# Paged attention with a conditional mix: other places for the new keys' second value products, the mix product and the weight loads

## The chip, the cores and the metric

The kernel runs on one core of a Trainium2 chip. The metric is the device time of one execution in microseconds (us). The engines of the core are named as the profile names them: PE (TensorE, matrix products), DVE (VectorE), ACT (ScalarE), POOL (GpSimd) and SP (SyncE, which here only issues transfers). Each has its own queue of instructions and works it off in order; they wait for each other through semaphores. SP, ACT and POOL each issue DMA transfers, in the order of their own instructions. [...]

## The reference, cut to what matters

```python
def _L0_cond_ref(x, weights, condition):             # x [64, 32, 512], weights [16, 32, 32]
    W = weights[condition]
    return jnp.einsum('bct,bcd->bdt', x, W)

def _L1_cond_ref(x, Wq, Wk, Wv, Wo, q_norm_w, k_norm_w, k_cache, v_cache, block_table, cache_seqlens):
    q = jnp.einsum('bsd,ed->bse', x, Wq).reshape(bsz, seqlen, HQ, D)     # 32 heads of 128
    k = jnp.einsum('bsd,ed->bse', x, Wk).reshape(bsz, seqlen, HK, D)     # 8 heads of 128
    v = jnp.einsum('bsd,ed->bse', x, Wv).reshape(bsz, seqlen, HK, D)
    q = _rope(_rmsnorm(q, q_norm_w), pos);  k = _rope(_rmsnorm(k, k_norm_w), pos)
    kc = k_cache[block_table].reshape(bsz, L, HK, D)                     # L = 512 cached keys
    vc = v_cache[block_table].reshape(bsz, L, HK, D)
    k_all = jnp.concatenate([kc, k], axis=1);  v_all = jnp.concatenate([vc, v], axis=1)
    scores = jnp.einsum('bqhd,bkhd->bhqk', q, repeat(k_all)) * SCALE     # masked by cache_seqlens
    o = jnp.einsum('bhqk,bkhd->bqhd', softmax(scores), repeat(v_all))
    return jnp.einsum('bse,de->bsd', o.reshape(bsz, seqlen, HQ * D), Wo)

x = x + _L0_cond_ref(x, L0_cond_weights, itok_B_0_15)
x = x + _L1_cond_ref(x, Wq, Wk, Wv, Wo, q_norm_w, k_norm_w, k_cache, v_cache, itok_Bx16_0_63, itok_B_207_1644)
```

All is float32. There are 64 batches of 32 tokens with 512 features. Each batch first mixes its 32 tokens by a 32x32 matrix that its condition picks out of sixteen ("the mix"), and then attends over 512 cached keys, which lie in pages, and its own 32 new ones.

## The kernel before

**Steps and batches.** A tile is 128 rows: four batches (BT = 4) of 32 tokens. There are 16 tiles (NT), and each is worked twice, once for each half of the heads (NHH = 2; 4 key heads, so 16 query heads, in a half): 32 steps. Steps 0 to 15 are the first half, 16 to 31 the second. The first half mixes x and stores its transpose and its sum in DRAM; the second loads them. A step runs its four batches one after the other (variable bt), and a batch its four key heads (variable g): 16 slots, slot = 4 bt + g.

**What a slot does.** The loop is at L834 to L892. Each slot has the scores of its own head against the cached keys (scores, L523: 4 products into ps, then an exponential on ACT into pr) and the value products of the head before (values, L579: 4 products into po; after each second head DVE adds the new keys' part nv, takes the reciprocal of the denominators and scales: L597 to L600). In between lie pieces of the next step (pieces, L803: mix and transpose of x, projections, norm and rotation, transposes) and of this one: new_scores (L538) in slot 0, new_values (L555) for heads 0 and 1 in slot 1 and for heads 2 and 3 in slot 3, and in slot 3 the output product of the step before (out_proj, L468, 32 products of 512 columns).

**Buffers in PSUM.** ps and po have two buffers each. Everything else on PE, the mix (pmix), x's transposes (px1t), projections (pp), their transposes (pt), new scores (psn), new values (pnv) and the output (pout), shares the tag "pp" with BT = 4 buffers. One call of new_values takes all four (one per batch); ACT copies each of them into nv (L577). nv has one buffer per step, so the first copies of a step wait until DVE has used the last values of the step before.

**Cached keys and values.** Keys come by SP as k_t, 16 transfers of 64 KB a batch, two batches deep (load_k, L265), issued when a Batch is made, two batches ahead. DVE copies one head of the following batch in each slot (head_keys, L514, into kh, four buffers). Values are gathered by POOL's indirect DMA (fetch, L296, into raw, three buffers), and ACT masks them into the batch's buffer (fill, L506 and mask_v, L313). Four fills come in slot 3 of each step, one in most others.

**Weights.** Each tag has one buffer. Wq, Wk, Wv of the second half are loaded in step 14 from slot 11 (L870), Wo of the first half in step 0, slots 9 to 12, Wo of the second in step 16, slots 12 to 15 (L868), all on SP's queue.

**The order of work.** PE's and SP's instructions run in the order of the program text (manual_schedule, L88). From the loop on, ACT, DVE and POOL are ordered by the scheduler of the framework, which follows the text by priority and by when it takes an instruction to be ready. Before the loop (L671 to L801, "the opening") all engines follow the text.

**The opening.** bd is a 128x128 matrix with the four 32x32 condition matrices on its diagonal; the mix product of a tile is bd against x. load_cond_weights (L241) loads the four condition numbers of a tile into registers and issues four transfers of 4 KB; in the opening it does so on ACT's queue.

Of the kernel before, what the change touches and what calls it, by code (L numbers as in the profile page):

```python
# [11 lines left out]
F32 = mybir.dt.float32  # L12
I32 = mybir.dt.int32
AF = mybir.ActivationFunctionType
ALU = mybir.AluOpType
# [4 lines left out]
P = 128  # L20
B, S, HID = 64, 32, 512
D, HQ, HK = 128, 32, 8
REP = HQ // HK
# [32 lines left out]
def cond_resid_paged_attention_kernel(  # L56
# [34 lines left out]


    cond_row = const.tile([1, NT, BT], I32, tag="cond", name="cond_row")
    lens_sb = const.tile([P, NT], I32, tag="lens", name="lens_sb")
    freq = const.tile([P, HD], F32, tag="freq", name="freq")
    norm_w = {}
# [88 lines left out]
    def steps_of(exact, pools):  # L185
# [34 lines left out]

        wt = {}

        def load_w(kind, hh, g=0):
            if kind == "q":
                src = wq[:, (hh * QH + g * REP) * D : (hh * QH + (g + 1) * REP) * D]
            elif kind == "o":
                src = wo[(hh * QH + g * REP) * D : (hh * QH + (g + 1) * REP) * D, :]
            else:
                src = (wk if kind == "k" else wv)[:, hh * GH * D : (hh + 1) * GH * D]
            t = wpool.tile(  # L230
                [P, 4, 512], F32, tag=f"w{kind}{g}", name=f"w{kind}{g}_{hh}_{uid}"
            )
            wt[kind, hh, g] = t
            if kind == "o" and not exact:
                src = src.rearrange("(h j p) e -> h p j e", h=REP, p=S)
                for h in range(REP):
                    nc.sync.dma_start(t[h * S : (h + 1) * S, :, :], src[h])
                return
            nc.sync.dma_start(t, src.rearrange("(c p) e -> p c e", p=P))

        def load_cond_weights(t, eng=nc.sync, kind=mybir.EngineType.SP):  # L241
            _, number = nc.values_load_multi_w_load_instructions(
# [99 lines left out]
        def x1_c(st):  # L342
            if st.hh:
                return
            pm = ps_p.tile([P, 512], F32, tag="pp", name=f"pmix_{st.name}")
            nc.tensor.matmul(pm, bd, st.acc, start=True, stop=True)  # L346
            nc.vector.tensor_tensor(st.acc, pm, st.acc, ALU.add)
# [322 lines left out]

        steps = [Step(n) for n in range(NHH * NT)]  # L671
        if not exact:
            nc.scalar.dma_start(cond_row, cond.rearrange("(i s) t -> s t i", s=S)[0:1])
            nc.gpsimd.dma_start(pages_sb, pages)
            nc.gpsimd.dma_start(norm_w["q"], qn_w.partition_broadcast(P))
            nc.gpsimd.dma_start(norm_w["k"], kn_w.partition_broadcast(P))
# [37 lines left out]
        load_w("q", 0, 0)  # L714
        nc.scalar.dma_start(lens_sb, lens)
        nc.scalar.dma_start(freq, inv_freq.partition_broadcast(P))
        load_cond_weights(0, nc.scalar, mybir.EngineType.Activation)
        load_w("k", 0)
        load_w("q", 0, 1)
        load_w("q", 0, 2)  # L720
# [81 lines left out]

        def pieces(st):  # L803
            do = {
                0: (x1_a, x1_c),
                3: (x1_b,),
                4: (k_a, (q_a, 0)),
                5: ((q_a, 1),),
                6: (v_a, k_b, (q_b, 0)),
                8: ((q_a, 2), (q_b, 1)),  # L810
                10: ((q_a, 3), (q_b, 2)),
                13: ((q_b, 3),),
            }
            if st is second:
                do[4], do[6] = ((q_a, 0),), (k_b, (q_b, 0))
            return do
# [17 lines left out]
        for st in steps:  # L834
# [4 lines left out]
            for bt in range(0 if st.n else 1, BT):  # L839
                this = batch  # L840
                for g in range(GH):
# [2 lines left out]
                        scores(this, g)  # L844
                    if slot == 0:
                        new_scores(st)
                    if slot == 1:
                        new_values(st, 0)
                    for piece in fill.get(slot, ()):
                        if isinstance(piece, tuple):  # L850
                            piece[0](ahead, piece[1])
                        else:
                            piece(ahead)
                    if slot == 3:
                        out_proj(steps[st.n - 1])
                        new_values(st, 2)
                        if st.n + 1 < NT // TRIG:
                            tmp = work.tile(
                                [P, 3, TRIG * HD], F32, tag="w1", name=f"trig_{st.n}"
                            )  # L860
# [110 lines left out]
```

## Time and profile before

| | |
|---|---|
| median of 4 runs (lowest to highest) | 2281.05 us (2277.68 to 2283.19) |
| the profiled execution: time, span | 2277.57 us, 2275.8 us |
| TensorE's granted clock, mean | 0.994 |
| PE busy in output products (L474), projections of q (L390) | 445.7, 460.6 us |
| PE busy in scores (L527), values (L585) | 542.5, 550.4 us |
| PE busy in new values (L569), mix (L346) | 62.2, 19.6 us |
| ACT busy in fills (L316), in exponentials (L535) | 361.7, 304.8 us |
| moved by DMA, mean rate | 318.13 MB, 140 GB/s |

The span is the time from the first to the last instruction of the profiled execution. Busy shares are averages over the span. A line of the timeline has the start and the length of an instruction or of a run of them in us, the engine, the line of the kernel, the operation, output and inputs, shape and count, and in brackets the idle time of the engine before it and what ended it. In a line of the list of waits stand the total, the number and the longest of the waits of one line for one other. Matrix products are pipelined: the starts of successive ones tell what one costs.

### The profile page before, as it was taken

To read this page: it belongs to the slowest core of one execution; us is meant where nothing else is said; L and a number is where in the kernel's file an instruction comes from. 1 tells how busy PE (TensorE), PEld (TensorE's weight loads), DVE (VectorE), ACT (ScalarE), POOL (GpSimd) and SP (SyncE) were. 2 spreads that over 40 slices of the span, in tenths; PEclk is the share of its full clock that TensorE was granted. 3 is DMA by queue.
4 is the path that set the end of the run, shared out by engine and by line. 5 is a ranking of instruction groups with operands and counts; after the bars stand their busy time and mean duration, and the time that the engine had idled before them with its cause. 6 is when DMAs were issued, how large, how long until landed. Compare 5 with 4: busy or idle time off the path is not lost.

```text
span 2275.8 us, 41860 instructions
## 1 busy us (share of the span) xinstructions
PE 2231.9 (98%) x13590; PEld 1566.1 (69%) x13590; DVE 1075.5 (47%) x2717; ACT 942.9 (41%) x1726; POOL 771.8 (34%) x1005
## 2 busy tenths in 40 slices
PE   8999999999999999999999999999999999999998
PEld 5766677666776667766677766677666777666775
DVE  4544455444454444554444544445534455444452
ACT  3444444444443344433344434344333444333442
POOL 3423333323333233332333323333333343333331
PEclk9999999999999999999999999999999999999999
DMA  7844454344443444435657444544344544344442
GB/s 220 198 131 126 138 150 128 110 132 139 143 135 115 136 136 139 138 119 160 206 150 185 143 121 129 150 139 138 113 134 132 148 148 121 112 137 142 144 134 68
DMA packets 364486, 318.13 MB, mean 140 GB/s; under 512 B 46737, under 2 KB 308881, under 8 KB 364257
## 3 DMA queue, kind: packets, MB, share of 16 engines
q1 hardware_dynamic: 320064, 176.53, 27.1%
q0 software_dynamic: 41136, 134.55, 19.6%
q10 hardware_dynamic: 3056, 4.27, 0.5%
q8 instruction: 110, 1.80, 0.3%
q14 instruction: 120, 0.97, 0.2%
HBM read 302.59 MB, written 12.58 MB: 138 GB/s over the span
## 4 chain that ended last, share of the span: by engine, by line
PE 88%; DMA 4%; DVE 3%; SPq 2%; issue 1%; ACT 1%; ACTq 0%; POOL 0%; DVEq 0%
PE pout_x L474 19%; PE pp_q_x L390 18%; PE po_x L585 18%; PE ps_x L527 17%; PE pp_v_x L390 5%; PE pp_k_x L390 5%; PE pt_q_x L434 2%; PE pnv_x L569 2%; SPq L279 2%; DMA raw_x<-in_vc_dram,v_row 1%; DMA wo_x<-in_wo_dram 1%; PE psn_x L545 1%; PE pmix_x L346 1%; PE pt_k_x L434 1%; DMA k_t_x<-in_kt_dram 1%
## 5 line engine op out<-in xcount | busy, mean ns | idle before, releaser
L303 POOL DMA_INDIRECT raw_x<-in_vc_dram,v_row x512 | 511.4, 999 | 675.3 <-ACT v_x L316 622.1
L585 PE MATMUL po_x<-v_x,pr_x 128*128 128x129 f32 x4096 | 550.4, 277 | 3.3 <-ACT pr_x L535 3.3
L527 PE MATMUL ps_x<-qt_x,kh_x 128*128 128x128 f32 x4096 | 542.5, 275 | 5.5 <-DVE kh_x L520 3.8
L585 PEld LDWEIGHTS po_x<-v_x,pr_x 128*128 128x128 f32 x4096 | 504.6, 192 | 51.3 <-issue 36.1
L527 PEld LDWEIGHTS ps_x<-qt_x,kh_x 128*128 128x128 f32 x4096 | 500.2, 192 | 7.9 <-issue 4.9
L535 ACT ACTIVATE pr_x<-ps_x 128x512 f32<-128x512 f32 x512 | 304.8, 600 | 379.7 <-PE ps_x L527 377.0
L390 PE MATMUL pp_q_x<-wq_x,x1t_x 128*128 128x512 f32 x1024 | 460.6, 592 | 0.0
L474 PE MATMUL pout_x<-wo_x,ot_x 128*128 128x512 f32 x1024 | 445.7, 593 | 2.9 <-ACT nv_x L577 2.7
L316 ACT ACTIVATE v_x<-raw_x,valid 128x512 f32<-128x512 f32 x512 | 361.7, 720 | 110.8 <-DMA raw_x<-in_vc_dram,v_row 110.3
L474 PEld LDWEIGHTS pout_x<-wo_x,ot_x 128*128 128x128 f32 x1024 | 191.9, 190 | 233.3 <-issue 229.1
L390 PEld LDWEIGHTS pp_q_x<-wq_x,x1t_x 128*128 128x128 f32 x1024 | 187.1, 190 | 198.5 <-issue 198.2
L520 DVE COPY kh_x<-k_t_x 128x512 f32<-128x512 f32 x506 | 215.9, 429 | 203.9 <-PE ps_x L527 113.1
L577 ACT COPY nv_x<-pnv_x 128x258 f32<-128x258 f32 x256 | 77.3, 388 | 341.2 <-PE pnv_x L569 276.4
L400 ACT ACTIVATE sq_q_x<-pp_q_x 128x512 f32<-128x512 f32 x128 | 76.5, 597 | 298.8 <-issue 133.1
L404 DVE TENSOR_REDUCE ms_q_x<-sq_q_x 128x4 f32<-128x512 f32 x128 | 87.3, 682 | 199.7 <-ACT sq_q_x L400 199.7
L407 POOL TENSOR_TENSOR rs_q_x<-ms_q_x,minus_half 128x4 f32<-128x4 f32 x128 | 132.5, 1035 | 129.9 <-DVE ms_q_x L405 129.7
L379 POOL TENSOR_TENSOR cw_k_x<-norm_k,cos 128x64 f32<-128x64 f32 x32 | 10.1, 315 | 442.1 <-DVE ms_k_x L405 442.1
L597 DVE TENSOR_TENSOR nv_x<-po_x,nv_x 128x258 f32<-128x258 f32 x256 | 107.5, 420 | 100.7 <-PE po_x L585 91.6
L411 DVE TENSOR_TENSOR rope_q_x<-pp_q_x,cw_q_x 128x512 f32<-128x512 f32 x128 | 87.3, 682 | 102.6 <-PE pt_k_x L434 102.6
L390 PE MATMUL pp_v_x<-wv_x,x1t_x 128*128 128x512 f32 x256 | 115.2, 592 | 0.0
L390 PE MATMUL pp_k_x<-wk_x,x1t_x 128*128 128x512 f32 x256 | 115.2, 592 | 0.0
L600 DVE TENSOR_TENSOR o_x<-nv_x,rden 128x256 f32<-128x256 f32 x256 | 107.8, 421 | 3.3
(95 smaller groups left out, 1426.1 us busy)
## 6 DMA issues: line engine op xcount, KB each, us to landing
k_t_x<-in_kt_dram SPq DMA_DIRECT2D x2048, 64.0 KB
wq_x<-in_wq_dram SPq DMA_DIRECT2D x8, 1024.0 KB
raw_x<-in_vc_dram,v_row POOLq DMA_INDIRECT x512, 3.9
wo_x<-in_wo_dram SPq DMA_DIRECT2D x32, 256.0 KB
xt_x<-in_x_dram SPq DMA_DIRECT2D x16, 256.0 KB
x1t_d<-x1t_x ACTq DMA_DIRECT2D x16, 256.0 KB
acc_d<-xt_x SPq DMA_DIRECT2D x16, 256.0 KB
acc_x<-acc_d SPq DMA_DIRECT2D x16, 256.0 KB
```

What stands on the lines that cost most here:

```text
L303: nc.gpsimd.indirect_dma_start(out=raw.rearrange("p g d -> p (g d)"), out_offset=None, in_=vc, in_offset=bass.IndirectOffsetOnAxis(ap=v_ro ...
L316: nc.scalar.activation(v_bufs[b % 2][:, c, :, 0:D], raw, AF.Copy, scale=ok)
L390: nc.tensor.matmul(pp, st.x1t[:, c, :], w[:, c, :], start=(c == 0), stop=(c == KC - 1))
L404: nc.vector.tensor_reduce(ms, sq, AX.X, ALU.add)
L407: nc.gpsimd.tensor_tensor(rs, ms, minus_half, ALU.pow)
L474: nc.tensor.matmul(po, st.ot[:, i, :], wt["o", st.hh, i // 4][:, i % 4, :], start=(i == 0), stop=(i == QH - 1),)
L520: last["dve"] = nc.vector.tensor_copy(k, ba.k_raw[:, :, g, :]).ins
L527: nc.tensor.matmul(ps[:, c, :], ba.k[g][:, c * P : (c + 1) * P], queries(ba, g), start=True, stop=True,)
L535: last["act"] = nc.scalar.activation(pr, ps, AF.Exp, scale=SCALE).ins
L585: nc.tensor.matmul(ba.po[:, g % 2, :], ba.pr[g][:, c, :], ba.v_t[:, c, g, :], start=(c == 0), stop=(c == VC - 1),)
L597: nc.vector.tensor_tensor(t, ba.po, t, ALU.add)
L600: nc.vector.tensor_tensor(ba.o[:, both, :], t[:, :, 0:D], rd.unsqueeze(2).to_broadcast([P, 2, D]), ALU.mult,)
```

## The change

Four things are done.

- new_values for heads 2 and 3 is called ahead of the other pieces of slot 3, and not behind the output product. In slots 0 to 3 the value products of the head before come ahead of the pieces, and not at the end of the slot. The mix product of the next step (x1_c) moves from slot 0 to the end of slot 2, and x's transposes (x1_b) stand in slot 3 behind the value products.
- load_w takes a part of a tile, and load_parts loads one half of a weight tile per slot. Wo is loaded in slots 4 to 11 of steps 0 and 16; Wk, Wq, Wv of the second half in slots 5 to 15 of step 14 and slot 0 of step 15.
- The mix weights of the first tile come by one indirect DMA on POOL: row numbers are computed on DVE from the first column of the conditions, the gather brings 128 rows of 32 values, and four copies (two on DVE, two on ACT) place them in bd.
- cond_row, which the other tiles' condition numbers are read from, is loaded on ACT's queue behind these copies.

```diff
+    cond_0 = const.tile([P, 1], I32, tag="cond_0", name="cond_0")
...
-        def load_w(kind, hh, g=0):
+        def load_w(kind, hh, g=0, part=slice(0, 4)):
...
-            t = wpool.tile(
-                [P, 4, 512], F32, tag=f"w{kind}{g}", name=f"w{kind}{g}_{hh}_{uid}"
-            )
-            wt[kind, hh, g] = t
+            if part.start == 0:
+                wt[kind, hh, g] = wpool.tile(
+                    [P, 4, 512], F32, tag=f"w{kind}{g}", name=f"w{kind}{g}_{hh}_{uid}"
+                )
+            t = wt[kind, hh, g]
...
-                for h in range(REP):
+                for h in range(part.start, part.stop):
                     nc.sync.dma_start(t[h * S : (h + 1) * S, :, :], src[h])
                 return
-            nc.sync.dma_start(t, src.rearrange("(c p) e -> p c e", p=P))
+            nc.sync.dma_start(t[:, part, :], src.rearrange("(c p) e -> p c e", p=P)[:, part, :])
+
+        def load_parts(which, hh, at):
+
+            if 0 <= at < 2 * len(which):
+                load_w(which[at // 2][0], hh, which[at // 2][1], slice(at % 2 * 2, at % 2 * 2 + 2))
...
-            nc.scalar.dma_start(cond_row, cond.rearrange("(i s) t -> s t i", s=S)[0:1])
+            nc.scalar.dma_start(cond_0, cond[:, 0:1])
+            nc.vector.tensor_scalar(cond_0, cond_0, float(S), row, ALU.mult, ALU.add)
...
-        load_cond_weights(0, nc.scalar, mybir.EngineType.Activation)
+        w_sel = work.tile([P, S], F32, tag="o", name="w_sel", bufs=1)
+        nc.gpsimd.indirect_dma_start(
+            out=w_sel,
+            out_offset=None,
+            in_=w_cond,
+            in_offset=bass.IndirectOffsetOnAxis(ap=cond_0, axis=0),
+        )
+        for i in range(BT):
+            blk = slice(i * S, (i + 1) * S)
+            (nc.scalar.copy if i % 2 else nc.vector.tensor_copy)(bd[blk, blk], w_sel[blk, :])
+        nc.scalar.dma_start(cond_row, cond.rearrange("(i s) t -> s t i", s=S)[0:1])
...
             do = {
-                0: (x1_a, x1_c),
-                3: (x1_b,),
+                0: (x1_a,),
...
-                    if slot == 1:
-                        new_values(st, 0)
+                    if slot in (1, 3):
+                        new_values(st, slot - 1)
+                    if slot < GH and valued is not None:
+                        values(*valued)
                     for piece in fill.get(slot, ()):
...
+                    if slot == 2 and ahead:
+                        x1_c(ahead)
                     if slot == 3:
+                        if ahead:
+                            x1_b(ahead)
                         out_proj(steps[st.n - 1])
-                        new_values(st, 2)
...
-                    if st.n == 0 and 9 <= slot < 13 or st.n == NT and slot >= 12:
-                        load_w("o", st.hh, (slot - 9 if st.n == 0 else slot - 12))
-                    if st.t == NT - 2 and st.hh + 1 < NHH:
-                        if slot == 11:
-                            load_w("k", st.hh + 1)
-                            load_w("v", st.hh + 1)
-                        if slot in (12, 13):
-                            for i in range(2):
-                                load_w("q", st.hh + 1, 2 * (slot - 12) + i)
+                    if st.t == 0:
+                        load_parts([("o", i) for i in range(GH)], st.hh, slot - GH)
+                    if st.n in (NT - 2, NT - 1):
+                        load_parts(
+                            [("k", 0), ("q", 0), ("q", 1), ("v", 0), ("q", 2), ("q", 3)],
+                            1,
+                            slot - 5 + (st.n - NT + 2) * BT * GH,
+                        )
...
-                    if valued is not None:
+                    if slot >= GH and valued is not None:
                         values(*valued)
```

More of the change, by code (lines that the diff above doesn't have):

```diff
@@ L853, in steps_of @@
                             piece(ahead)
+                    if slot == 2 and ahead:
+                        x1_c(ahead)
                     if slot == 3:
+                        if ahead:
+                            x1_b(ahead)
                         out_proj(steps[st.n - 1])
-                        new_values(st, 2)
                         if st.n + 1 < NT // TRIG:
-                            tmp = work.tile(
-                                [P, 3, TRIG * HD], F32, tag="w1", name=f"trig_{st.n}"
-                            )
+                            tmp = work.tile([P, 3, TRIG * HD], F32, tag="w1", name=f"trig_{st.n}")
                             with tc.issue_after(last["dve"]), tc.issue_after(last["act"]):
```

## The prediction

> **What bounds the kernel now.** I read the busy shares first, then TensorE's waits, then the order of time in one ordinary step and in the places that the waits point to. Busy shares:
>
> ```profile
> PE 2231.9 (98%) x13590; PEld 1566.1 (69%) x13590; DVE 1075.5 (47%) x2717; ACT 942.9 (41%) x1726; POOL 771.8 (34%) x1005
> ```
>
> TensorE (PE) sets the time. The change neither adds nor removes a matmul, so it can only act on time in which PE stands or is slow: 44 us of the 2275.8 us span look idle. TensorE's list of waits, at its places:
>
> ```profile
> PE pmix_x L346 <- DMA bd<-in_w_cond_dram: 8.0, 1, 8.0
> PE pnv_x L569 <- DVE xt_x L481: 5.7, 16, 0.4
> PE pnv_x L569 <- DVE acc_x L481: 5.3, 15, 0.4
> PE ps_x L527 <- DVE kh_x L520: 3.8, 1, 3.8
> PE po_x L585 <- ACT pr_x L535: 3.3, 1, 3.3
> ```
>
> Each edit aims at one of these. The second and third come once in every step from 1 on. The timeline of step 8 (PE's rows, slot 1 above, slot 3 below the dots):
>
> ```profile
> 604.91 1.06 PE L527 MATMUL ps_x<-qt_x,kh_x 128*128 128x128 f32 x8
> 605.89 0.73 PE L569 MATMUL pnv_x<-vn_x,pn_x 32*128 32x129 f32 x16
> 606.55 1.16 PE L585 MATMUL po_x<-v_x,pr_x 128*128 128x129 f32 x8
> 607.55 1.06 PE L527 MATMUL ps_x<-qt_x,kh_x 128*128 128x128 f32 x8
> ...
> 610.66 13.90 PE L474 MATMUL pout_x<-wo_x,ot_x 128*128 128x512 f32 x32
> 624.49 0.50 PE L569 MATMUL pnv_x<-vn_x,pn_x 32*128 32x129 f32 x6
> 625.35 0.71 PE L569 MATMUL pnv_x<-vn_x,pn_x 32*128 32x129 f32 x10 [0.36 <-DVE xt_x L481]
> 625.98 1.16 PE L585 MATMUL po_x<-v_x,pr_x 128*128 128x129 f32 x8
> 626.98 1.06 PE L527 MATMUL ps_x<-qt_x,kh_x 128*128 128x128 f32 x8
> ```
>
> Start to start, the same sixteen matmuls take 0.66 us in slot 1 and 1.49 us in slot 3: new_values takes all four "pp" buffers of PSUM (BT = 4), and the fourth still holds the output product until VectorE (DVE) has added it. So 0.83 us are lost, twice what the wait list books.
>
> The end of step 0, all engines but the weight loads:
>
> ```profile
> 102.52 1.06 PE L585 MATMUL po_x<-v_x,pr_x 128*128 128x129 f32 x8
> ...
> 106.78 1.43 DVE L520 COPY kh_x<-k_t_x 128x512 f32<-128x512 f32 x4 [3.86 <-DMA wo_x<-in_wo_dram]
> 107.36 2.05 PE L527 MATMUL ps_x<-qt_x,kh_x 128*128 128x128 f32 x8 [3.78 <-DVE kh_x L520]
> 109.33 1.94 PE L545 MATMUL psn_x<-qt_x,kn_x 128*32 128x128 f32 x32
> ```
>
> The keys of the next batch stood behind 4 MB of Wo on SP's queue, and after the wait PE ran slowly (psn 1.94 us against 1.08 in step 8).
>
> **New keys (steps 1 to 31).** I call t0 the start of a step's slot-0 scores (start of psn less 0.98 us) and L the time after t0 at which DVE copies the first keys of batch 1. DVE is in order, and this copy waits for k_t. In step 4:
>
> ```profile
> 323.58 0.69 DVE L347 TENSOR_TENSOR xt_x<-pmix_x,xt_x 128x512 f32<-128x512 f32 x1 [3.31 <-PE pmix_x L346]
> 327.45 0.43 DVE L520 COPY kh_x<-k_t_x 128x512 f32<-128x512 f32 x1 [3.18 <-DMA k_t_x<-in_kt_dram]
> 328.96 1.21 ACT L577 COPY nv_x<-pnv_x 128x258 f32<-128x258 f32 x4 [2.94 <-DVE o_x L600]
> ```
>
> Behind that copy stands the normalising of the last batch, and only then may ScalarE (ACT) overwrite nv and free the four buffers of slot 1's new_values. L is 7.0 us here; over steps 2 to 14 it is 5.2 to 7.0, mean 6.4; over 16 to 31 5.4 to 7.5 where it shows.
>
> Before, PE goes from pout's start to slot 4's scores in 13.75 us of product and a 2.57 us tail (624.41 to 626.98). After, the tail's work stands ahead of pout at slot 1's pace: 0.75 new_values with its gap, 0.99 values.
>
> Steps whose successor is in the second half (15 to 31, no mix): pout starts at t0 + 8.31 when nothing waits, so 8.31 + 2.57 = 10.88 becomes 8.31 + 1.74 = 10.05: 0.83 us saved. If L is late, slot 1's copies end at L + 2.3 (step 19: L 6.2, ended at 8.5), the new product at L + 2.75, values at L + 3.75; for L = 7.5 that is 11.25, against 9.57 + 2.57 before (step 23). The saving stays 0.8 to 0.9. 17 steps by 0.83: **14.1 us**.
>
> Steps 1 to 14: the mix product moves from slot 0 to the end of slot 2, and with it its DVE sum. There it asks for a pp buffer while slot 1's new_values holds all four. Copies start L + 1.05 (as in step 19, where the order in slot 0 is already the new one), the first is out at L + 1.45. Then mix 0.97, scores 0.89, new_values 0.75, values 0.99, x transposes 0.44: pout at L + 5.5. The fourth pnv tile also waits for the mix's sum, which stands on DVE behind the copies and the normalising of slot 2 (about L + 3.9 at its end); I add 0.2. L + 5.7 with L = 6.4 is 12.1; before, 9.60 + 2.57 = 12.17. So **0**: the old wait is paid, the new one takes its place. Bounds per step: 0.83 gained (nothing waits), 1.1 lost (the sum stands behind one more key copy and L is 7.0).
>
> ACT is the other cover: pout (or the x transposes) now needs a copy of slot 3's new values, and four v fills are ready in the same slot. In slot 0 one fill already goes ahead of the copy of psn's result. A fill takes 0.62 of ACT's time (two in a row: 1.33, one: 0.71); in a second-half step with one ahead, the first copy ends at scores' end + 0.69 + 0.62 + 0.39 = 1.7 us, when values has ended too (1.74). One is free; each further one costs 0.62. I take one; bounds none and four.
>
> **Wo in halves.** In step 0 the 16 transfers go to slots 4 to 11. SP stands still from 60.3 to 66.4 us with the DMA share at 0.03 (60 to 65), so 2 MB fit before batch 3's keys; the other 2 MB follow them, and batch 4's keys can be issued from about 84 instead of 86.8 to 102, needed at 94 by DVE. Without the stall psn would start at 104.4 instead of 109.33 and the next po, now at 112.91, at 106.28: **6.6 us**. In step 16 the same 16 transfers delay v's gathers (5.6 us wait on ACT, then 3.3 on PE); the distance from that pout to the next is 73.71 against 68.86: **4.85 us**. Now they are spread over about 37 us of long slots. Cover gone (keys or gathers late all the same): both stay, 11.5 us.
>
> **Wk, Wv, Wq** go in twelve halves over slots 5 to 15 of step 14 and slot 0 of 15. Before, step 15 loses 0.78 us (69.64 against 68.86). Behind the halves on SP stand batch 3's and the next step's keys; the last 2 MB come just ahead of those for batch 1 of step 15. I take 0.4 saved; bounds 0.8 saved, 5 lost (2 MB at 296 GB/s are 7 us, 2 of them in time that SP has).
>
> **The opening.** Removed: four register loads and four 4 KB transfers on ACT's queue, whose last lands at 15.6. Added: a 512 B column, one DVE operation (0.15 us, like the row computation on a 128x1 tile), a gather, four 32x32 copies (each under a 128x128 DVE operation's 0.23 or ACT's 0.40). The column lands about 4.5 to 5.5 (cond_row was read at 3.9; lens, later, landed at 7.2), the gather is issued by 6.8 (1 us on POOL). Its landing is not in the trace: bounds 3.9 (median of v's gathers over the whole run) and 8.5 (lens_at, issued among the same loads), and I take 6.5, nearer to the latter for its place: 13.3, bd at 13.7, 2 us sooner.
> [...]
> Behind the waiting gather on POOL stand pages_at and lens_at: issued at 7 instead of 3.4, landing by 15.5, needed at 19.0. Behind the copies on DVE stands the first angle table, which can't start before 11.55 anyway, and the mix's sum behind it; cond_row's second use on ACT is at 22.1. Then batch 0's keys, issued until 31.05, and Wv, issued at 31.1, meet a PE that comes sooner, so I keep **1 us**; bounds 5 saved, 2 lost.
>
> Sum: 14.1 + 0 + 6.6 + 4.85 + 0.4 + 1 = 27 us. The profiled execution took 2277.57 us (span 2275.8), so it would be 2250.6; it was 3.5 below the median of the runs shown, 2281.05, so the median goes to **2254 us**.
>
> **Rivals.**
> A. Steps 1 to 14 gain too (L falls, or the copies come sooner): 14 by 0.83 more is 11.6: 2242. For it: L below 5.7 in steps 9, 12 and 13. Against: ten others.
> B. Two or three fills ahead of the copies on ACT: the 17 steps lose 0.62 or 1.24 each, 14 more about 0.4: 2270 to 2281. For it: raws for three fills wait in slot 3, and after x's copy three fills do run in a row there. Against: that copy went ahead of them.
> C. The halves only move the stall: 11.5 back, 2265.
> D. Slower: all four fills ahead. The fourth waits for a gather started by the first (step 8: it ends 16.1 us after t0, step 18: 14.4), so pout starts 0.4 later: 4.3 lost in 14 steps, 3.9 in 17, together 127 against 13 saved elsewhere: 2395. It decides from the third fill on, where the steps lose more than they gain. Against: its gather lands long after the new product.
>
> **How the numbers follow.** Chances: forecast 0.45 (2248 to 2261), A 0.17, B 0.18, C 0.08, D 0.12. Range 2240 to 2276: it leaves out D, the top of B and the bottom of A. Under 0.2% (4.6 us) this kernel's runs, 2277.68 to 2283.19, can't tell from no change. Faster: forecast, A, C and most of B, 0.83; same 0.04; slower 0.13.
>
> **What would show it.** Right: pnv's waits for xt and acc gone; pmix or pnv waiting for nv copies or for xt's sum in steps 2 to 14, with a step distance near 70.1 there and near 68.0 after 17; no wait of ps at 103 us; nothing over 70 us between pouts of steps 16 and 17. Wrong: x's transposes or pout waiting for nv (fills ahead), distances of 69.3 already in steps 2 to 14 (A), or the k_t copies of step 15 later than t0 + 11.

## The result and the profile after

The changed kernel takes 2282.76 us (median of 35 runs, 2276.5 to 2289.2) against 2281.28 us (56 runs, 2276.4 to 2285.5): ratio 1.0008, interval 1.0002 to 1.0014. The forecast was 2254 us, in a range of 2240 to 2276. The profiled execution has a span of 2280.2 us against 2275.8. The whole expected gain is missing.

The busy shares of the changed kernel:

```profile
PE 2232.5 (98%) x13590; PEld 1570.4 (69%) x13590; DVE 1074.4 (47%) x2720; ACT 939.3 (41%) x1727; POOL 779.6 (34%) x1006
```

Its list of TensorE's waits (lines of the changed kernel stand 7 further down: the output product is L481, the nv copies L584):

```profile
PE pout_x L481 <- ACT nv_x L584: 9.7, 17, 0.7
PE pmix_x L353 <- ACT bd L734: 7.6, 1, 7.6
PE ps_x L534 <- DVE kh_x L527: 4.2, 2, 2.3
PE pnv_x L576 <- DVE xt_x L354: 3.8, 5, 0.9
PE pnv_x L576 <- ACT nv_x L584: 3.5, 4, 1.2
PE pmix_x L353 <- ACT nv_x L584: 3.1, 4, 1.3
PE px1t_x L361 <- ACT nv_x L584: 2.1, 7, 0.4
```

The waits of the new value products for the output's sum (5.7 and 5.3 us before) are gone, as forecast. In their place stand waits for the nv copies: 17 of the output product, one in each of the 17 steps that the forecast had put down as saved, and 15 of the mix, the new values and x's transposes.

Step 23 shows the first kind (PE's and ACT's rows of slot 3, timeline of the changed kernel):

```profile
1660.03 0.73 PE L576 MATMUL pnv_x<-vn_x,pn_x 32*128 32x129 f32 x16
...
1660.69 1.16 PE L592 MATMUL po_x<-v_x,pr_x 128*128 128x129 f32 x8
1660.69 1.32 ACT L323 ACTIVATE v_x<-raw_x,valid 128x512 f32<-128x512 f32 x2
...
1661.91 1.19 ACT L584 COPY nv_x<-pnv_x 128x258 f32<-128x258 f32 x4
1662.32 4.13 PE L481 MATMUL pout_x<-wo_x,ot_x 128*128 128x512 f32 x9 [0.48 <-ACT nv_x L584]
```

The new values were finished at about 1660.7. ACT then ran two fills, 1.32 us, and copied only at 1661.91; the output product, which needs a buffer that the first copy frees, started at t0 + 10.69 instead of the forecast 10.05.

Step 3 shows the others (the same view):

```profile
255.02 1.13 PE L353 MATMUL pmix_x<-xt_x,bd 128*128 128x512 f32 x2 [0.34 <-ACT nv_x L584]
...
257.62 0.71 ACT L323 ACTIVATE v_x<-raw_x,valid 128x512 f32<-128x512 f32 x1
258.35 0.71 PE L576 MATMUL pnv_x<-vn_x,pn_x 32*128 32x129 f32 x10 [0.88 <-DVE xt_x L354]
258.36 1.28 ACT L149 ACT_TABLE_LOAD   x1
...
259.65 0.31 ACT L149 ACTIVATE sin<-trig 128x128 f32<-128x128 f32 x1
259.87 1.18 ACT L584 COPY nv_x<-pnv_x 128x258 f32<-128x258 f32 x4
...
260.77 2.74 PE L481 MATMUL pout_x<-wo_x,ot_x 128*128 128x512 f32 x6
```

The mix in slot 2 waits for the slot 1 copies, the fourth buffer of new values waits for the mix's sum, and then a fill, a table load and a sine of the next angles stand ahead of the copies. The step is 71.64 us long, against 70.15 before.

Below, t0 is used as in the prediction (the start of psn less 0.98 us), and a step's length is the distance to the next t0. From the psn rows of each timeline come the stretches of every kernel that was run, in us; the runs are told of in the next section:

| kernel | start to step 2 | steps 2 to 14 | 15 to 17 | 18 to 30 | step 31 to end | span |
|---|---|---|---|---|---|---|
| before | 180.1 | 912.0 | 212.2 | 900.9 | 70.6 | 2275.8 |
| after | 176.0 | 919.8 | 206.7 | 904.1 | 73.5 | 2280.2 |
| e1 copies first | 177.6 | 913.5 | 207.4 | 887.8 | 71.0 | 2257.3 |
| e2 and mix in slot 0 | 175.9 | 903.0 | 205.5 | 889.4 | 71.3 | 2245.0 |
| e3 mix in slot 0 alone | 177.5 | 914.2 | 210.1 | 898.2 | 73.9 | 2273.9 |
| e4 before, loads in halves | 177.8 | 913.2 | 209.3 | 904.9 | 70.9 | 2276.0 |
| e5 e2, Wo of step 0 later | 177.6 | 903.4 | 209.7 | 891.0 | 71.2 | 2252.9 |
| e6 e2, keys behind turn | 177.2 | 902.8 | 207.1 | 884.3 | 73.8 | 2245.2 |
| e7 moves alone | 180.8 | 922.9 | 214.0 | 902.9 | 74.7 | 2295.2 |
| e8 before, new opening | 175.3 | 912.4 | 214.9 | 905.9 | 69.7 | 2278.2 |
| e9 after, one fill ahead | 178.2 | 914.6 | 205.5 | 895.2 | 73.2 | 2266.6 |
| e10 before, keys behind turn | 177.9 | 912.3 | 212.7 | 900.0 | 70.0 | 2272.8 |
| e11 e6, old loads and opening | 180.6 | 902.5 | 213.4 | 884.6 | 70.9 | 2252.0 |

### The profile page after: what moved, and what is told of

It reads as the page before. It is cut to its first block, busy times and chain, and to the rows that moved or that the text cites. A ratio compares the mean times of both kernels' runs of the same rounds, so it can differ in the third digit from the quotient of the medians.

```text
span 2280.2 us, 41900 instructions
## 1 busy us (share of the span) xinstructions
PE 2232.5 (98%) x13590; PEld 1570.4 (69%) x13590; DVE 1074.4 (47%) x2720; ACT 939.3 (41%) x1727; POOL 779.6 (34%) x1006
## 4 chain that ended last, share of the span: by engine, by line
PE 76%; DMA 7%; SPq 6%; ACT 4%; issue 4%; DVE 3%; ACTq 0%; DVEq 0%
PE pout_x L481 20%; PE pp_q_x L397 17%; PE ps_x L534 13%; PE po_x L592 12%; SPq L286 5%; PE pp_v_x L397 5%; PE pp_k_x L397 5%; DMA k_t_x<-in_kt_dram 4%; PE pt_q_x L441 2%; ACT v_x L323 1%; ACT nv_x L584 1%; ACT pr_x L542 1%; DMA acc_x<-acc_d 1%; DMA wo_x<-in_wo_dram 1%; DVE kh_x L527 1%
## 5 line engine op out<-in xcount | busy, mean ns | idle before, releaser
L481 PE MATMUL pout_x<-wo_x,ot_x 128*128 128x512 f32 x1024 | 448.0, 596 | 9.7 <-ACT nv_x L584 9.7
L481 PEld LDWEIGHTS pout_x<-wo_x,ot_x 128*128 128x128 f32 x1024 | 192.7, 191 | 242.7 <-issue 229.6
L386 POOL TENSOR_TENSOR cw_k_x<-norm_k,cos 128x64 f32<-128x64 f32 x32 | 10.1, 316 | 442.4 <-DVE ms_k_x L412 442.4
L488 DVE TENSOR_TENSOR xt_x<-pout_x,xt_x 128x512 f32<-128x512 f32 x16 | 11.1, 692 | 250.3 <-PE pout_x L481 250.3
L488 DVE TENSOR_TENSOR acc_x<-pout_x,acc_x 128x512 f32<-128x512 f32 x16 | 11.1, 692 | 233.5 <-PE pout_x L481 233.5
```

What stands on the lines that cost most here:

```text
L481: nc.tensor.matmul(po, st.ot[:, i, :], wt["o", st.hh, i // 4][:, i % 4, :], start=(i == 0), stop=(i == QH - 1),)
```

## The experiments

**e1, the nv copies ahead of fills and angles.** The theory: two fills (in steps 2 to 6 one fill and the angles) ahead of slot 3's copies on ACT take the gain.

```diff
-                nc.scalar.copy(st.nv[:, bt, g0 : g0 + 2, :], pv[bt])
+                last["act"] = nc.scalar.copy(st.nv[:, bt, g0 : g0 + 2, :], pv[bt]).ins
```

(Fills and angles are issued behind last["act"].)

> The changed kernel, with the copies of slot 3's new values put ahead of the v fills and the angle tables on ACT. Theory 'ACT order': in the changed kernel two fills (and in steps 1 to 6 a table load) run ahead of these copies, and the output product waits for the first of them. Then here, in steps 16 to 31, the output product starts at t0 + 10.05 to 10.1 where the keys are in time (10.70 in the changed kernel), the distance of such steps falls from 68.77 to about 68.15 us, and in steps 7 to 9, 12 and 13 from 70.0 to about 69.4; in all about 17 us less, 2264 us. Theory 'late keys': what holds the output product is DVE behind the copy of batch 1's keys; then the copies' order changes nothing, distances stay at 68.8 and 70.0 and the time at 2281 to 2283 us.

Measured: 2260.65 us, ratio 0.9918 (0.9893 to 0.9943). Step 23, from the timeline of this kernel:

```profile
1649.13 0.60 ACT L542 ACTIVATE pr_x<-ps_x 128x512 f32<-128x512 f32 x1 [0.20 <-PE ps_x L534]
...
1649.71 1.21 ACT L584 COPY nv_x<-pnv_x 128x258 f32<-128x258 f32 x4
1650.62 3.60 PE L481 MATMUL pout_x<-wo_x,ot_x 128*128 128x512 f32 x8
1650.78 1.97 ACT L323 ACTIVATE v_x<-raw_x,valid 128x512 f32<-128x512 f32 x3
```

The copies run as soon as the new values are there, and the output product stands waiting for nothing. In the second half it starts at t0 + 10.05 and the step is 68.02 us long, the forecast's numbers, in every step whose keys land in time (step 22, with late keys, took 69.78). The order on ACT is the cause in the second half. Steps 2 to 14 fall from 919.8 to 913.5 us, which is only where they stood before.

**e2, also the mix back in slot 0.** Behind the new scores, where all buffers are free.

```diff
                     if slot == 0:
                         new_scores(st)
+                        if ahead:
+                            x1_a(ahead)
+                            x1_c(ahead)
...
-                    if slot == 2 and ahead:
-                        x1_c(ahead)
```

> As the run before, and the mix product back in slot 0, ahead of the values, where it stood before the change. Theory 'mix in slot 2 waits': steps 2 to 14 pay for the mix product's wait for a pp buffer and for its sum on DVE; then here their output products start at t0 + 11.3 to 11.5 in all of them (12.05 to 13.67 in the changed kernel) and the distance is 69.3 to 69.4; with the run before's gain in the second half about 28 us less than the changed kernel, 2254 us. Theory 'late keys': steps with keys after t0 + 6 keep 70.5 to 71.6, and the time stays above 2270 us.

Measured: 2249.49 us, 0.9869 (0.9846 to 0.9893). Steps 2 to 14 take 903.0 us, 69.46 each on the mean, 69.32 where nothing is late. Step 3 of this kernel (timeline):

```profile
247.21 1.13 PE L353 MATMUL pmix_x<-xt_x,bd 128*128 128x512 f32 x2
...
254.83 0.73 PE L576 MATMUL pnv_x<-vn_x,pn_x 32*128 32x129 f32 x16
...
255.57 1.21 ACT L584 COPY nv_x<-pnv_x 128x258 f32<-128x258 f32 x4
256.48 0.60 PE L361 MATMUL px1t_x<-ident,xt_x 128*128 128x128 f32 x4
```

Mix, new values and transposes run without a wait: the place of the mix cost 10.6 us over steps 2 to 14 (913.5 to 903.0).

**e3, the mix alone back in slot 0**, ACT's order as in the changed kernel.

```diff
-                0: (x1_a,),
+                0: (x1_a, x1_c),
...
-                    if slot == 2 and ahead:
-                        x1_c(ahead)
```

> The changed kernel with only the mix product back in slot 0; fills still ahead of the copies. Theory 'two separate waits': steps 7 to 14 all go to 70.0 (10, 11 and 14 were at 71.6, 71.5 and 70.5), steps 2 to 6 keep about 70.8 (fill and table load ahead), the second half keeps 68.77; about 5 us less than the changed kernel, 2277 us. If the mix product's wait and the fills hide each other's cost, the gain of the run before's pair is not the sum of the two and this run is at 2281 us or above.

Measured: 2275.61 us, 0.9970 (0.9956 to 0.9984); steps 2 to 14 914.2. The output product waits for nv as before (9.7 us, 17 times), and x's transposes now too (7.4 us, 14 times). So each edit alone brings steps 2 to 14 back to about the old 912, and only both together make them shorter: with the mix out of the way, ACT's order ends last, and the other way round.

**e4, the kernel before with the halves alone** (load_w with its part, and):

```diff
-                    if st.n == 0 and 9 <= slot < 13 or st.n == NT and slot >= 12:
-                        load_w("o", st.hh, (slot - 9 if st.n == 0 else slot - 12))
...
+                    if st.t == 0:
+                        load_parts([("o", i) for i in range(GH)], st.hh, slot - GH)
+                    if st.n in (NT - 2, NT - 1):
+                        load_parts(
...
```

> The kernel before with only the weight loads in halves. Theory 'the halves do half of what was forecast': step 16 to 17 falls from 73.71 to 68.9 us; in step 0 the wait for keys at 103 us goes, but another of some 2 to 4 us comes near 77 or 96 us, since DVE's order puts the key copies of batch 3 behind the rotations; about 6 us less than before, 2275 us. The forecast's view: no wait in step 0 at all, 11.5 us less, 2270 us.

Measured: 2276.73 us, 0.9986 (0.9974 to 0.9997): 3.2 us, of 11.85 forecast for the loads. Steps 15 to 17 gain 2.9 us against the profile before. From the start of step 0 to that of step 2 it takes 119.1 us, and with the old loads 118.9 (e8), 119.0 (e10), 121.4 (e7) and 121.5 (before, e11), 120.5 on the mean. The seven profiles with these halves have 119.1 to 121.2, 120.0 on the mean: no difference that stands out of the spread.

**e5, Wo of step 0 in slots 8 to 15**, on e2.

```diff
-                        load_parts([("o", i) for i in range(GH)], st.hh, slot - GH)
+                        load_parts([("o", i) for i in range(GH)], st.hh, slot - (2 * GH if st.n == 0 else GH))
```

> The second experiment's kernel with one edit: the halves of Wo of step 0 are issued in slots 8 to 15 of that step instead of slots 4 to 11. Theory 'two halves of Wo stand ahead of batch 3's keys on SP': in the runs with halves, step 0 waits about 2 us at its queries' transposes and about 2 us each at batch 3's key copies (50.0 us in the second experiment, where a step without such waits would be about 45). With Wo behind the keys: step 0 about 45 to 46 us, no wait of products for key copies in it above 0.5 us, the whole about 4 to 5 us under the second experiment (ratio to before 0.985). Theory 'the transfers of step 0 are full whatever the order' (their share is about 1.0 from 64 to 92 us): the waits move to a later batch or to step 1, and the whole stays within 1 us of the second experiment (0.987).

Measured: 2253.34 us, 0.9876 (0.9856 to 0.9895), not to be told from e2's 0.9869. Step 0 falls to 44.89 us, as the first theory has it, and step 1 rises from 69.32 to 76.12. There, in the timeline of this kernel:

```profile
108.81 0.72 ACT L323 ACTIVATE v_x<-raw_x,valid 128x512 f32<-128x512 f32 x1 [2.32 <-DMA raw_x<-in_vc_dram,v_row]
110.06 0.73 PE L576 MATMUL pnv_x<-vn_x,pn_x 32*128 32x129 f32 x16 [3.70 <-ACT pn_x L560]
```

A fill waits for its gather, behind it on ACT stand the new keys' weights pn, and PE waits 3.70 us. The wait has moved from keys to gathers: the second theory. In the changed kernel the DMA share is 1.03 from 64 to 78 us and 1.05 from 78 to 92; there is no room in which Wo would be free. Over all thirteen profiles steps 0 and 1 together last 118.9 to 121.5 us, whichever way Wo comes.

**e6, the keys behind the turn**, on e2. In slots 0 and 1 DVE copies the next batch's first keys, and when they land late the sums and the turn of the outputs wait behind them, and with them the output product.

```diff
-                    if later is not None:
-                        head_keys(later, g)
+                    if later is not None and not (slot == 0 and turned is not None):
+                        if slot == 1:
+                            with tc.issue_after(last["turn"]):
+                                head_keys(later, 0)
+                                head_keys(later, 1)
+                        else:
+                            head_keys(later, g)
```

> The second experiment's kernel with one edit: the copies of batch 1's first two heads' keys are issued on VectorE in slot 1 behind the turn of the outputs, instead of in slots 0 and 1 ahead of it. Theory 'late keys hold VectorE': a step in which these keys land late (later than about 6.2 us from its start) has the new values' sums and the turn behind the copies, and so a late output projection; these steps are 69.3 to 70 us instead of 68.02 in the second half and up to 0.7 over 69.32 in the first. With the edit every step of the second half is 68.0 to 68.1 and every one of the first 69.3 to 69.4, whenever its keys land, and the whole is 4 to 6 us under the second experiment (ratio to before about 0.985). Theory 'the scores themselves want the keys': the same steps stay long, now with waits of the scores for the key copies, and the whole stays within 1 us of the second experiment.

Measured: 2243.83 us, 0.9837 (0.9822 to 0.9851), the fastest version. Steps 18 to 30 take 884.3 us, 13 by 68.02, whenever the keys land; of steps 2 to 14, two stay 0.5 and 0.8 us over 69.32. Step 21 of this kernel (timeline):

```profile
1495.53 0.71 DVE L617 STREAM_TRANSPOSE ot_x<-o_x 128x512 f32<-128x512 f32 x1
...
1498.14 1.10 DVE L527 COPY kh_x<-k_t_x 128x512 f32<-128x512 f32 x3 [1.90 <-DMA k_t_x<-in_kt_dram]
...
1501.27 1.02 PE L481 MATMUL pout_x<-wo_x,ot_x 128*128 128x512 f32 x2
```

The keys land 6.9 us after t0 (1491.22), and the output product still starts at t0 + 10.05. By the ratios e6 is 7 us faster than e2, by intervals that overlap a little; the two profiled executions have the same span, since what steps 18 to 30 gain here (5.1 us) the start, steps 15 to 17 and step 31 lose (1.3, 1.6 and 2.5).

**e7, the moves within the slots alone**, with the opening and the loads of the kernel before; against the changed kernel:

```diff
-                        load_parts([("o", i) for i in range(GH)], st.hh, slot - GH)
+                    if st.n == 0 and 9 <= slot < 13 or st.n == NT and slot >= 12:
+                        load_w("o", st.hh, (slot - 9 if st.n == 0 else slot - 12))
...
-        w_sel = work.tile([P, S], F32, tag="o", name="w_sel", bufs=1)
...
+        load_cond_weights(0, nc.scalar, mybir.EngineType.Activation)
```

> The kernel before with the change's moves within the slots alone (value products ahead of the mix and the fills in slots 0 to 3, mix sum's product in slot 2, second new values first in slot 3); opening and weight loads as before. Theory 'the moves lose what the other parts gain': steps 2 to 14 about 70.4 on the mean (70.15 before), about 68.8 in the second half, the step after the loads of Wk, Wv and Wq 73.7 as before: 4 to 9 us over before, ratio 1.002 to 1.004. Theory of the forecast for the moves (0.83 in each of 17 steps gained, nothing in the first half): 14 us under before, ratio 0.994.

Measured: 2294.63 us, 1.0056 (1.0038 to 1.0074). By the ratio the moves alone lose 12.8 us, more than expected. In the profile, whose span is 19.4 us longer, steps 2 to 14 have 10.9 of it, steps 15 to 17 1.8, steps 18 to 30 2.0 and the last one 4.1. The forecast had the moves gain 14.

**e8, the new opening alone**, on the kernel before.

```diff
-        load_cond_weights(0, nc.scalar, mybir.EngineType.Activation)
+        w_sel = work.tile([P, S], F32, tag="o", name="w_sel", bufs=1)
+        nc.gpsimd.indirect_dma_start(
...
+        nc.scalar.dma_start(cond_row, cond.rearrange("(i s) t -> s t i", s=S)[0:1])
```

> The kernel before with the change's opening alone: the first conditions' weights by one gather of 128 rows and eight copies into the diagonal, instead of register loads and eight transfers. Theory 'the whole gain of the opening reaches step 0': the changed kernel's step 0 began 1.83 us earlier; step 0's own length is unchanged by it, and the end comes 1.8 us earlier (ratio 0.9992). Theory 'step 0 is bounded by its transfers': step 0 begins 1.8 us earlier and is as much longer, because its keys and Wo land when they did before, and the whole is within 0.5 us of before (1.000).

Measured: 2280.46 us, 1.0001 (0.9989 to 1.0012): inconclusive, since both expectations lie in the interval. (The edit has four copies in place of four transfers, not eight.) By the profiles the opening is worth about 2 us up to step 0: t0 of step 0 is at 56.4 to 57.6 us in the eight profiles that have the new opening, 58.6 to 59.3 in the five with the old, and step 2 starts 2.5 us earlier on the mean (176.9 against 179.4; seven of the eight have the halves too, of the five only e4).

**e9, one fill ahead instead of two**, on the changed kernel: the other fills and the angles are issued behind the copies.

```diff
+                last["nv"] = nc.scalar.copy(st.nv[:, bt, g0 : g0 + 2, :], pv[bt]).ins
...
+            with tc.issue_after(last["act"]), tc.issue_after(last[behind]):
                 ba.fill(c)
...
+                        for i in range(1 if bt or g == 0 else VC):
+                            next_values("nv" if i and "nv" in last else "act")
```

> The changed kernel with one fill of values ahead of slot 3's nv copies on ScalarE instead of two: the other fills and the angles are issued behind the copies; nothing else is moved. Theory 'one fill is free, the second costs': the output projection of the second half starts 10.05 us after the step's start and its steps are 68.02 us, as in the first experiment with none ahead; no wait of the projection for nv; together with the angles that no longer stand ahead in steps 1 to 6 the whole is the first experiment's 2260.7 us, up to 2 us off. Theory 'already the first fill costs': 10.3 to 10.4 us and 68.4, a wait of 0.3 us for nv in each of 17 steps, the whole about 2268 us.

Measured: 2268.45 us, 0.9935 (0.9916 to 0.9955). Step 26 of this kernel (timeline):

```profile
1860.17 0.72 ACT L323 ACTIVATE v_x<-raw_x,valid 128x512 f32<-128x512 f32 x1
1860.79 1.19 ACT L584 COPY nv_x<-pnv_x 128x258 f32<-128x258 f32 x4
1861.21 1.99 PE L481 MATMUL pout_x<-wo_x,ot_x 128*128 128x512 f32 x4
```

With one fill ahead the output product starts at t0 + 10.09 and a step is 68.16 us long in time for its keys: the first fill costs 0.14, the second 0.61 (68.77 in the changed kernel). By the steps this is the first theory; the whole, however, is 2268 and not 2261. The stretches show where: steps 18 to 30 are 7.4 us longer than in e1, of which 13 by 0.14 are 1.8, and the rest are steps with late keys. In the three longest of them (18, 19 and 22) slot 1's copies wait for DVE, which stands behind keys that land 6.8 to 7.8 us after t0. That part differs from run to run (see below). The intervals of the two ratios overlap, and the whole time alone fits the second theory (2268); what separates them is the 0.14 us of the steps in time, where that theory has 0.4.

**e10, the kernel before with e6's edit alone** (the same diff).

> The kernel before with the sixth experiment's edit alone (copies of batch 1's first two heads' keys behind the turn). Theory 'late keys hold VectorE in the kernel before too': steps 18 to 30 are 68.86 us each (68.85 to 70.20 before, 69.4 on the mean), the first half stays at 70.15 where its steps already stood; about 6 to 8 us less than before, ratio 0.997. Theory 'only the new order is sensitive to the keys': same as before, 1.000.

Measured: 2275.15 us, 0.9973 (0.9959 to 0.9986), 3 to 9 us less. The first theory has the sign and nearly the size, but that the late keys made the difference isn't shown: in this profile steps 18 to 30 gain only 0.9 (900.0 against 900.9). Ten of them stand at 68.9 to 69.2, three (23, 26 and 29) at 69.9 to 70.5. In these three PE stops in the middle of slot 1's scores, with no wait that the profile shows ("issue"). Step 23 (PE's rows):

```profile
1650.48 0.87 PE L527 MATMUL ps_x<-qt_x,kh_x 128*128 128x128 f32 x6
1652.30 0.39 PE L527 MATMUL ps_x<-qt_x,kh_x 128*128 128x128 f32 x2 [0.95 <-issue]
```

Between the sixth and the seventh of eight products PE stands for 0.95 us; in step 26 it is two such stops of 0.80 us together, in step 29 two of 0.37. e8 has them in the same place in steps 20, 23, 26 and 29 (0.45, 0.60, 0.97 and 0.53 us), the profiles before and after have nothing of the kind in steps 2 to 31. What they are stays open.

**e11, e6 with the old opening and the old loads** (e7's diff, on e6).

> The sixth experiment's kernel with the opening and the weight loads of the kernel before: the new order in the slots with nv copies first, mix in slot 0 and the keys behind the turn. Theory 'halves and opening are worth here what they were in the kernel before': 3.2 us and 0.3 us more than the sixth experiment, about 2247 us; the step after Wo's second load is 73 to 75 us, the other steps of the second half 68.02. Theory 'the faster the steps, the more the halves save': step 17 above 75 us and the whole 2250 us or more.

Measured: 2251.29 us, 0.9864 (0.9848 to 0.9880), 7.5 us more than e6. Step 17 takes 76.00 us against 68.02, the second theory. In this kernel's timeline (here the value products are L585, the new values L569):

```profile
1223.98 0.72 ACT L316 ACTIVATE v_x<-raw_x,valid 128x512 f32<-128x512 f32 x1 [4.52 <-DMA raw_x<-in_vc_dram,v_row]
1225.24 1.16 PE L585 MATMUL po_x<-v_x,pr_x 128*128 128x129 f32 x8 [2.67 <-ACT pr_x L535]
```

Wo in one piece delays the gathers of step 16, a fill waits 4.52 us, behind it on ACT an exponential, behind that PE.

## Why the prediction was wrong

The forecast's terms against the profiles, by stretches (us, minus is a gain):

| stretch | forecast | measured |
|---|---|---|
| start to step 2: opening 1, Wo of step 0 6.6 | -7.6 | -4.1 |
| steps 2 to 14 | 0 | +7.8 |
| steps 15 and 16: 2 by 0.83, Wk, Wv, Wq 0.4 | -2.1 | -0.6 |
| step 17: 0.83, Wo of step 16 4.85 | -5.7 | -4.9 |
| steps 18 to 30: 13 by 0.83 | -10.8 | +3.3 |
| step 31 | -0.8 | +2.9 |
| sum | -27.0 | +4.4 |

**The step that failed: "in a second-half step with one ahead ... One is free; each further one costs 0.62. I take one."** Two were ahead in each of the 17 steps. The price was right: the second fill cost 0.61, and it left 0.09 of the 0.83 us (68.77 against 68.86). The first, taken as free, cost 0.14. What failed is the count, which was read off another slot with another row in it: the copy of psn's result in slot 0. e1 and e9 are the changed kernel but for this order, and their output products start at the forecast's 10.05 and at 10.09. By the mechanism this is rival B, which was given 0.18; its condition was named among the things that would show the forecast wrong. It explains 17 by 0.74, 12.6 of the 31.4 us between the two sums. With two fills ahead B gives 2270, its lower end; the other 12.8 us up to 2282.76 lie in the terms below.

**Steps 1 to 14: "The old wait is paid, the new one takes its place. So 0."** The mechanism was there (the mix waiting for copies, the fourth buffer for the mix's sum), and with the copies first the size is nearly right: 913.5 against 912.0 in e1. What was left out is that ACT's order acts here as well, with the sine's table load in place of the second fill in steps 2 to 6: 6.3 us (919.8 to 913.5). e2 shows that the wait could be avoided: in slot 0 the mix waits for nothing, and these steps gain rival A's 0.83 (69.32 against 70.15).

**Wo of step 0: 6.6.** Near zero: 0.5 between the means told under e4, in a spread of 2.6. The halves took the wait at 103 us away and put others in its place; the changed kernel's step 0 has Wo, keys and Wo in turn on SP, and this (PE's, DVE's and SP's rows):

```profile
58.70 5.01 SPq L239 DMA_DIRECT2D wo_x<-in_wo_dram  x8
65.00 10.48 SPq L286 DMA_DIRECT2D k_t_x<-in_kt_dram  x16
75.52 4.64 SPq L239 DMA_DIRECT2D wo_x<-in_wo_dram  x8
...
97.64 1.54 DVE L527 COPY kh_x<-k_t_x 128x512 f32<-128x512 f32 x4
98.20 1.13 PE L534 MATMUL ps_x<-qt_x,kh_x 128*128 128x128 f32 x8 [2.29 <-DVE kh_x L527]
```

The sum "2 MB fit before batch 3's keys" looked at SP's idle time and not at what the 16 DMA engines already had to move in those 28 us (DMA share 1.03 from 64 to 78 us, 1.05 from 78 to 92). This half of the loads is rival C ("the halves only move the stall"), and e5 shows it from the other side.

**Wo of step 16: 4.85.** Right: step 17 became 4.94 us shorter. The transfers had room here: before, the DMA share was 0.33 from 1175 to 1190 us and 0.26 from 1190 to 1205, but 1.05 from 1220 to 1232; in the changed kernel it is 0.55, 0.85 and 0.51. With the old order of the slots the halves save 4.0 over steps 15 to 17 (e4 against the mean of before, e8 and e10), with the new one 6.2 (the mean of seven profiles against e7 and e11).

**Wk, Wv, Wq: 0.4.** Not to be told apart: steps 15 and 16 gained 0.6 in all.

**The opening: 1.** The gather landed at 13.0 us, against the forecast 13.3, but that is luck: it was issued at 4.58 instead of by 6.8, and took 8.4 us instead of 6.5. ACT's copies had a table load of 1.28 us ahead of them, which wasn't in the sum, so bd was done at 14.76 instead of 13.7. t0 of step 0 moved 1.8 us. The cover that was feared to be thin (keys, Wv) held but for one wait of 0.41 us for Wv.

**What was not in the sum: late keys.** Steps 18 to 30 lost 3.3 us, although the order itself gains 1.2 (13 by 0.09). Counted as what exceeds the steps' standing length (68.86 before, 68.77 after), other things took 5.7 us of the profile before and 10.1 of the one after. In the changed kernel 8.0 of the 10.1 lie in the four steps whose first keys of batch 1 land later than 7 us after t0 (18, 19, 24 and 27). Step 19, the longest (72.21 us; t0 is 1372.45):

```profile
1380.61 0.43 DVE L527 COPY kh_x<-k_t_x 128x512 f32<-128x512 f32 x1 [4.55 <-DMA k_t_x<-in_kt_dram]
1381.66 1.21 ACT L584 COPY nv_x<-pnv_x 128x258 f32<-128x258 f32 x4 [4.48 <-DVE o_x L607]
1382.09 1.54 PE L576 MATMUL pnv_x<-vn_x,pn_x 32*128 32x129 f32 x16 [1.18 <-ACT nv_x L584]
```

The keys land 8.2 us after t0, the normalising stands behind their copy on DVE, ACT's copies behind that, and PE behind these. Over e3, e4, e7 and e8, which have one or the other of these orders, the excess was 4.2, 9.7, 8.9 and 10.8 (in e8 2.5 of it are the stops told under e10): no mark of the change, but a spread of some us between runs of one order. e6 and e11 reduce it to 0.0 and 0.4.

**What was not in the sum: step 31.** It was to gain 0.83 and lost 2.9 us. This goes with the new order. SP's rows, before (t0 is 2205.22) and after (2206.68):

```profile
2228.96 0.35 SPq L486 DMA_DIRECT2D out_dram<-acc_x  x1
2231.03 8.60 SPq L279 DMA_DIRECT2D k_t_x<-in_kt_dram  x16
...
2232.13 0.35 SPq L493 DMA_DIRECT2D out_dram<-acc_x  x1
2234.21 8.73 SPq L286 DMA_DIRECT2D k_t_x<-in_kt_dram  x16
```

The store of step 30's output stands on SP ahead of the last keys. Since the new values now come ahead of the output product, this product starts at t0 + 10.70 instead of 9.01; the store goes out at t0 + 25.45 instead of 23.74, the keys behind it 1.7 us later too, and the scores wait 1.92 us for their copy (the wait at 2247.59 below). In both profiles the keys go out 2.1 us after the store. All nine profiles with the new order have such a wait in step 31, of 1.46 to 2.70 us, and the four with the old order (before, e4, e8 and e10) have none; no run moved the store alone. The steps before have projections there; step 31 has none. It ends 69.7 to 70.9 us after its t0 in the old order and 70.9 to 74.7 in the new.

**The parts together.** By the ratios the moves lose 12.8 us (8.7 to 16.9) and the halves save 3.2 in the old order; together that is 9.6, or 7.8 more than the changed kernel's 1.8. Of these, 2.3 are what the halves save more over steps 15 to 17 in the new order, and 2 can be the opening's. The rest is not explained; the intervals are wide enough for it.

What stays open: why the framework's scheduler set two fills ahead in slot 3 and one in slot 0 wasn't tried, and e8 leaves open whether the opening's 2 us reach the end.

## What to carry to other kernels

When a matrix product is moved nearer to the copies that free its buffers, write the copies' place on their engine into the program, or count from the order as issued what will stand ahead of them; an order seen in one slot is no evidence for another. A gain that is bounded by two engines in turn shows only when both are mended: e1 and e3 each brought steps 2 to 14 back to where they were, e2 gained 9 us there. Where transfers were full (step 0, DMA share 1.03 and 1.05 in the changed kernel), spreading them moved a wait to the next consumer; where they had room (step 16, 0.33 and 0.26 before), it removed it. Whoever moves a product also moves the store of its result, and with it what stands behind that store on its queue (step 31: the store 1.71 us later, the keys behind it 1.7).

## What the runs showed of the hardware

**A gather under load.** The opening's gather of 128 rows (16 KB), in the timeline of the changed kernel:

```profile
4.58 1.04 POOL L726 DMA_INDIRECT w_sel<-in_w_cond_dram,cond  x1 [1.18 <-DVE cond L681]
13.03 1.28 ACT L734 ACT_TABLE_LOAD   x1 [13.03 <-DMA w_sel<-in_w_cond_dram,cond]
...
14.32 0.44 ACT L734 COPY bd<-w_sel 32x32 f32<-32x32 f32 x2
14.78 1.28 ACT L149 ACT_TABLE_LOAD   x1
```

It landed 8.4 us after its issue, at the upper of the forecast's bounds. And ahead of the two copies on ACT stands a table load of 1.28 us, between the landing and bd; ahead of the sine behind them stands another, 1.28 us at 14.78. Before, where no copy stands ahead of the first sine, there is one load up to that sine, 1.28 us at 9.83.

**The clock after a wait.** Two waits for keys in the changed kernel, of 2.29 us at 98.20 and of 1.92 us at 2247.59. The windows behind them (PE's busy time, the other engines', then the granted clock, the DMA share and the rate):

```profile
98.00:100.00 2.00, 1.80 (x16) 1.83 (x17) 1.18 (x4) 0.58 (x2) 0.29 (x1) 1.00 0.42 125
...
2247.60:2250.00 2.40, 2.40 (x13) 2.40 (x14) 0.85 (x3) 0.64 (x2) 0.00 (x0) 0.58 0.00 0
```

The longer wait left the clock at 1.00, the shorter one was followed by 0.58. The first eight products after them took 1.13 and 1.68 us. In finer windows of the changed kernel the clock is 1.00 from 2244.58 to 2247.98, with PE busy for 1.48 of the 3.40 us, then 0.50 from 2248.00 to 2251.39 with PE busy throughout, and 1.00 again from 2251.41. The seven changes of the clock in this trace lie whole multiples of 3.413 us apart (12.26, 19.08, 1384.41, 1387.83, 2247.99, 2251.40 and 2275.30). Here neither the length of a wait nor PE's busy time just ahead settles whether the clock drops: in the 3.41 us up to the end of the longer wait (94.79 to 98.20) PE is busy for 1.12 us and the clock stays at 1.00, in the 3.40 us ahead of the drop at 2247.99 PE is busy for 1.48 and ahead of the one at 1384.41 for 2.31. What settles it these traces do not show.
